# A graph layer's first product as seven block products, and norms applied one stage after their statistics

## The chip, the core and the metric

The kernel runs on one core of a Trainium2 chip. The metric is device time in microseconds for one launch; the table below has the runs. A core has TensorE (PE in the profile; its weight loads are PEld), VectorE (DVE), ScalarE (ACT), GpSimd (POOL) and SyncE (SP), each with an instruction queue of its own, and 16 DMA engines. All data is 32-bit float.

## The reference, cut to what matters

`x` is 128 graphs of 64 nodes with 256 features, `adj` their 64x64 weighted adjacency. Four layers follow each other, and each ends in `x = layernorm(x + layer(x, adj))`. Layer 0 takes five groups of the first 25 nodes (25, 9, 7, 6 and 6 nodes). For each group `g`:

```
def _graph_conv(x, adj, W, b):
    A = adj + eye
    norm_adj = dinv[:, :, None] * A * dinv[:, None, :]
    return relu(norm_adj @ (x @ W) + b)
...
h     = _graph_conv(x_g, adj_g, W1[g], b1[g])      # 256 -> 512
out_g = _graph_conv(h,   adj_g, W2[g], b2[g])      # 512 -> 256
fused[:, idx] += norm_w[g] * out_g
```

Nodes 25 to 63 belong to no group: in layer 0 they only get the layer norm. Layer 1 is one such convolution, layer 2 a polynomial in the adjacency, and layer 3 five rounds of messages and a GRU cell, which take most of the time.

## The kernel before, in words

**Units.** Layer 0 is cut into 16 units (`Unit`, L42; `UNITS`, L61), numbered from 0. A unit is up to four tiles of up to 126 rows of one group; a tile's rows are all nodes of the group in some graphs. The groups come in the order 1, 2, 3, 4, 0: units 0 to 2 are group 1 (504, 504 and 144 rows), 3 and 4 group 2 (448 each), 5 and 6 group 3 (504, 264), 7 and 8 group 4 (504, 264), 9 to 15 group 0 (500 each, the last 200). Units 6 and 8 have tiles of 126, 126 and 12 rows.

**Stages of a unit.** `load0` (L345) loads adjacency and features. `prep` (L367) forms the normalized adjacency of each tile on VectorE, with a power on GpSimd (`inv_sqrt`, L116), transposes it on TensorE (L399) and evicts it as `AT` (L403). `aggregate` (L406) multiplies features and adjacency (L413) and copies the result to `ag0`, which has 2 blocks of 128 features by the unit's rows as columns. `hidden` (L421) is the first product: `hg` has 4 blocks of 128 hidden features; each is the sum of two products of a 128x128 block of `W1` with a block of `ag0` (L428), 8 matmuls over all columns, then a relu with bias on ScalarE (L432). `support` (L436) is the second product, two tiles to a PSUM bank (L444), copied by ScalarE (L450). `add` (L457) multiplies by the adjacency again (L466) with a relu (L470) and adds into `F`. For group 0, `finish` (L491) transposes back, adds and norms, and stores to `xa` (L514).

**Order.** TensorE's order is the order of the code (`manual_schedule`, L332). The other engines' orders are set by a planner that works with priorities; `high_priority` raises them, and `issue_after(ins)` keeps instructions behind `ins` on that engine. `evictions[-1]` is the last L403 traced. The loop at L581 goes over stages `i`, each with `add(i-1)`, `aggregate(i+1)`, `support(i)`, `finish(i-1)`, `prep(i+2)`, `hidden(i+1)`. From stage 10 on, `early_stage` weaves the start of layers 1 and 2 for the first two chunks (`mid`, L220) in between; its L210 is the first to read `xt`.

**PSUM.** There are eight banks, five in the pool `pg` and three in `pt`; `psum0` (L181) takes five of eight in turn from `pg` and three from `pt`.

**Other nodes.** Groups of up to four nodes pass through `load_others` (two stages ahead), `others` (L522) and `store_others` (L527) to `xb` in DRAM. `norm_stats` (L128) takes statistics on VectorE and a power on GpSimd (L139), `norm_apply` (L146) subtracts and scales on VectorE (L154). `load_x` (L194) reads `xa` and `xb` back by SyncE (L199); it is first called at stage 10. The last two groups are normed in stage 9 and stored in stage 10.

**Weights.** `load_first` (L549) and `load_second` (L552) bring a group's `W1` and `W2`, 512 KB each, by one DMA on SyncE, into tiles that hold all five groups; all are loaded by stage 4.

**Layer 3** already forms a product of 2x2 blocks by seven block products: `sums` (L714) on GpSimd, `factors` (L681) on VectorE, and `Gates` (L722), whose `product(i)` multiplies (L737), copies partial sums out of PSUM on ScalarE (L754), and adds on VectorE (L756, L760, L766).

Of the kernel before, what the change touches and what calls it, by code (L numbers as in the profile page):

```python
# [68 lines left out]
def gnn_stack(  # L69
# [117 lines left out]


    def load_adj(c):
        a64 = keep.tile([128, NP, N], F32, name="a64", bufs=2)  # L190
        nc.sync.dma_start(a64, av[c])
        adjs[c] = a64
# [142 lines left out]
    with ExitStack() as c0:  # L335
        w0 = c0.enter_context(tc.tile_pool(name="w0", bufs=1))
        work = c0.enter_context(tc.tile_pool(name="work0", bufs=1))
        W1 = w0.tile([128, NG, 2, HID], F32, name="W1")
        W2 = w0.tile([128, NG, 4, D], F32, name="W2")

        F = w0.tile([128, 2, B, NE], F32, name="F")

        loads, A, AG, HG, S2, Z, XO = {}, {}, {}, {}, {}, {}, {}

# [75 lines left out]

        def hidden(i):  # L421
            u = UNITS[i]
            ag0 = AG.pop(i)
            hg = keep.tile([128, 4, 512], F32, tag="NI", name="hg", bufs=2)
            for e in range(4):
                p = psum0("ph")[:, : u.cols]
                for k in range(2):
                    nc.tensor.matmul(  # L428
                        p, W1[:, u.g, k, e * 128 : (e + 1) * 128], ag0[:, k, : u.cols], start=k == 0, stop=k == 1
                    )  # L430
                relus.append(
                    nc.scalar.activation(hg[:, e, : u.cols], p, AF.Relu, bias=b1[:, u.g * 4 + e : u.g * 4 + e + 1])  # L432
                )
            HG[i] = hg

        def support(i):  # L436
            u = UNITS[i]
            hg, s2 = HG.pop(i), []
            for v in range(0, len(u.tiles), 2):
                p = psum0("ps").rearrange("p (t d) -> p t d", t=2)  # L440
                ts = range(v, min(v + 2, len(u.tiles)))
                for t in ts:
                    for e in range(4):
                        nc.tensor.matmul(  # L444
                            p[: u.rows[t], t - v, :], hg[:, e, u.off[t] : u.off[t] + u.rows[t]], W2[:, u.g, e, :],
                            start=e == 0, stop=e == 3,
                        )
                sv = work.tile([TR, 2, D], F32, name="s2", bufs=4)
                if u.rows[ts[0]] == u.rows[ts[-1]]:
                    nc.scalar.copy(sv[: u.rows[v], : len(ts), :], p[: u.rows[v], : len(ts), :])  # L450
                else:
                    for t in ts:
                        nc.scalar.copy(sv[: u.rows[t], t - v, :], p[: u.rows[t], t - v, :])
                s2 += [sv[:, t - v, :] for t in ts]
            S2[i] = s2
# [66 lines left out]
        def others(i):  # L522

            with tc.issue_after(evictions[-1].ins):
                layernorm(XO[i], n=XO[i].shape[1])

        def store_others(i):  # L527
            t = XO.pop(i)
            nc.sync.dma_start(xb[:, NP * i : NP * i + t.shape[1], :], t)

# [18 lines left out]
        def load_first(g):  # L549
            nc.sync.dma_start(W1[:, g], w1[g].rearrange("(k p) e -> p k e", p=128))  # L550

        def load_second(g):  # L552
            nc.sync.dma_start(W2[:, g], w2[g].rearrange("(k p) e -> p k e", p=128))

# [21 lines left out]
        def stage(f, i, first=0):  # L576
            if first <= i < NU:
                f(i)

        g0 = next(i for i, u in enumerate(UNITS) if u.g == 0)  # L580
        for i in range(-2, NU + 1):  # L581
            if i >= 0:
                stage(load0, i + 3)
            stage(add, i - 1)
            if i:
                stage(aggregate, i + 1)
            early_stage(i, 0)
            stage(support, i)
            if not i:
                aggregate(1)  # L590
            if i == NU:
                folds = [products(0, q) for q in range(3)]
            stage(finish, i - 1, g0)
            early_stage(i, 1)
            if i == -1:

                hidden(0)
                with tc.issue_after(evictions[0].ins):
                    prep(1)
            else:  # L600
                stage(prep, i + 2)
                stage(hidden, i + 1)
            if i == -2:
                load0(1, powers[0])
                load_second(1)
                load0(2, powers[0])
                load_first(2)
            elif i == -1:
                load_second(2)
                load_first(3)  # L610
            elif i == 0:
                load_second(3)
            elif i < 5:
                (load_first, load_second)[(i - 1) % 2]((4, 0)[(i - 1) // 2])
            early_stage(i, 2)
# [56 lines left out]


    WHH = work.tile([128, 3, 7, 128], F32, name="WHH")
    V = [work.tile([128, 3, 7, 128], F32, name=f"V{l}") for l in range(L)]

    raw21 = []

    raw21 = []

    def factors(w):  # L681

        nc.vector.tensor_sub(w[:, :, 5, :], w[:, :, 4, :], w[:, :, 0, :])
        nc.vector.tensor_sub(w[:, :, 2, :], w[:, :, 1, :], w[:, :, 5, :])

    def fold():
# [7 lines left out]
        for l in range(L):  # L694
            for q in range(3):
# [12 lines left out]
                if q == 2 and l == 0:  # L708
                    nc.vector.tensor_add(WHH[:, :, 4, :], w21, WHH[:, :, 3, :])
                    nc.vector.tensor_sub(WHH[:, :, 6, :], WHH[:, :, 0, :], w21)  # L710
                    factors(WHH)
                yield

    def sums(a, name):  # L714

        t = work.tile([128, 4, H], F32, tag="T" + name, name="T" + name, bufs=2)
        nc.gpsimd.tensor_sub(t[:, 0:2, :], a[:, :, H:], a[:, 0, :].rearrange("p (s n) -> p s n", s=2))  # L717
        nc.gpsimd.tensor_sub(t[:, 2, :], a[:, 1, H:], t[:, 0, :])
        nc.gpsimd.tensor_sub(t[:, 3, :], a[:, 1, :H], t[:, 2, :])
        return t  # L720

    class Gates:  # L722

        def __init__(self, C, sides, name):
            self.C, self.sides, self.name = C, sides, name
            self.copies = {}

        def multiply(self, bank, i):  # L730
            for g, side in enumerate(self.sides):
                for m, (w, q, a, t) in enumerate(side):
                    rhs = {
                        1: a[:, 0, :H], 2: a[:, 1, :H], 3: a[:, 1, H:], 4: t[:, 3, :], 5: t[:, 0, :], 6: t[:, 2, :],
                        7: t[:, 1, :],
                    }[i]
                    nc.tensor.matmul(  # L737
                        bank[:, g, :], w[:, q, i - 1, :], rhs, start=i in (1, 2, 5) and g == 0 and m == 0,
                        stop=m == len(side) - 1, skip_group_check=True,
                    )  # L740

        def bank(self, s):
            return pg.tile([128, 2, H], F32, tag="pg", name=f"p{s}{self.name}")

        def product(self, i):
            C = self.C
            if i == 1:
                self.a = self.bank("a")
            if i in (1, 6, 7, 4):
                self.multiply(self.a, i)  # L750
                if i != 4:
                    c = self.copies[i] = work.tile([128, 2, H], F32, tag="copy", name=f"c{i}", bufs=4)
                    with tc.high_priority():
                        nc.scalar.copy(c, self.a)  # L754
                if i == 7:
                    nc.vector.tensor_add(C[:, :, 1, H:], self.d, self.copies.pop(7))  # L756
            elif i == 2:
                b = self.bank("b")
                self.multiply(b, i)
                nc.vector.tensor_add(C[:, :, 0, :H], b, self.copies.pop(1))  # L760
            else:
                if i == 5:
                    self.d = self.bank("d")
                self.multiply(self.d, i)
                if i == 3:
                    nc.vector.tensor_add(C[:, :, 0, H:], self.d, self.copies.pop(6))  # L766

    class Chunk:
# [12 lines left out]
        def state_of_layer2(self, k):  # L781
# [4 lines left out]
            if not k:  # L786
                self.th = sums(self.hT, "h")

        def messages(self, h=None):
            self.agg = gather(self.xt if h is None else h, self.A01, "agg", work, "agg", 2)  # L790
            self.ta = sums(self.agg, "a")

        def rz(self, i):
            if i == 1:
                self.RZ = keep.tile([128, 2, 2, NP * 128], F32, tag="RZ", name="RZ", bufs=2)
                self.g = Gates(
                    self.RZ, [[(WHH, q, self.hT, self.th), (V[self.l], q, self.agg, self.ta)] for q in (0, 1)], "rz"
                )
# [11 lines left out]
        def n(self, i):  # L810
            if i == 1:
                self.NI = keep.tile([128, 2, 2, NP * 128], F32, tag="NI", name="NI", bufs=2)
                self.gn = Gates(
                    self.NI, [[(V[self.l], 2, self.agg, self.ta)], [(WHH, 2, self.hT, self.th)]], "n"
                )
# [61 lines left out]
        def turn(self, k):  # L877
# [9 lines left out]
            if not last:  # L887
                with tc.high_priority():
                    nc.scalar.copy(self.h[:, :, f], pv)
                if not k:  # L890
                    self.th = sums(self.hT, "h")
            else:
# [159 lines left out]
```

## Time and profile before

| what | value |
|---|---|
| three runs | 2195.18, 2197.6, 2195.16 us (median 2195.18) |
| profiled run, its span | 2195.32 us, 2193.5 us |
| layer 0 | about the first 300 us of the span |
| TensorE, share of busy time, 0 to 100 us and 100 to 200 us | 97%, 100% |
| VectorE, 100 to 200 us | 48% |
| ScalarE, 100 to 200 us | 37% |
| GpSimd, 100 to 200 us | 16% |
| DMA, mean share of 16 engines, 0 to 20 us and 160 to 180 us | 0.87, 0.15 |

A row of the view of groups has line, engine, operation, output and input tiles, shape and count, then busy time and the mean of one in ns, then the idle time before it and what ended it. A row of the timeline has the start, the time from the first start to the last end, and the count. `SPq` is SyncE's queue, in which DMAs are issued. A window's row has its bounds, its length, then busy time and count of PE, PEld, DVE, ACT and POOL, then TensorE's granted clock, the share of the DMA engines and GB/s.

### The profile page before, as it was taken

To read this page: it belongs to the slowest core of one execution; us is meant where nothing else is said; L and a number is where in the kernel's file an instruction comes from. 1 tells how busy PE (TensorE), PEld (TensorE's weight loads), DVE (VectorE), ACT (ScalarE), POOL (GpSimd) and SP (SyncE) were. 2 spreads that over 40 slices of the span, in tenths; PEclk is the share of its full clock that TensorE was granted. 3 is DMA by queue.
4 is the path that set the end of the run, shared out by engine and by line. 5 is a ranking of instruction groups with operands and counts; after the bars stand their busy time and mean duration, and the time that the engine had idled before them with its cause. 6 is when DMAs were issued, how large, how long until landed. Compare 5 with 4: busy or idle time off the path is not lost.

```text
span 2193.5 us, 30145 instructions
## 1 busy us (share of the span) xinstructions
PE 2177.2 (99%) x11542; PEld 1907.7 (87%) x11542; DVE 1362.9 (62%) x3060; ACT 1001.2 (46%) x1839; POOL 571.2 (26%) x621
## 2 busy tenths in 40 slices
PE   9999999999999999999999999999999999999997
PEld 6777888898988889888989888888898898888886
DVE  3445666566766576666666676657666666556546
ACT  3333334544544554444444454445444544455453
POOL 3211131222332222222322222222322222222221
PEclk9999999999999999999999999999999999999998
DMA  6532110000100010000000010001000000000000
GB/s 166 180 120 67 49 37 3 1 3 1 42 1 3 1 41 2 3 1 20 22 3 1 1 42 1 3 1 42 1 1 1 20 10 1 1 10 11 1 1 20
DMA packets 54172, 51.12 MB, mean 23 GB/s; under 512 B 20878, under 2 KB 49036, under 8 KB 54028
## 3 DMA queue, kind: packets, MB, share of 16 engines
q1 hardware_dynamic: 49664, 43.96, 6.5%
q0 software_dynamic: 1936, 4.83, 0.8%
q8 instruction: 91, 1.49, 0.3%
q10 hardware_dynamic: 2428, 0.41, 0.1%
q14 instruction: 53, 0.43, 0.1%
HBM read 32.40 MB, written 16.78 MB: 22 GB/s over the span
## 4 chain that ended last, share of the span: by engine, by line
PE 96%; DVE 1%; issue 1%; POOL 0%; ACT 0%; DMA 0%; SPq 0%; POOLq 0%; ACTq 0%; DVEq 0%
PE parz L737 25%; PE pdrz L737 12%; PE pan L737 12%; PE pa L210 9%; PE pbrz L737 6%; PE pdn L737 6%; PE ps L444 4%; PE ph L428 4%; PE pT L778 4%; PE pbn L737 3%; PE pd L288 3%; PE pd L309 2%; PE pa L413 1%; PE po L466 1%; PE pf L562 1%
## 5 line engine op out<-in xcount | busy, mean ns | idle before, releaser
L754 ACT COPY c<-parz 128x512 f32<-128x512 f32 x240 | 140.6, 586 | 323.3 <-PE parz L737 322.7
L737 PE MATMUL parz<-Th,WHH 128*128 128x256 f32 x960 | 285.9, 379 | 0.3 <-ACT c L754 0.3
L737 PE MATMUL parz<-Ta,V 128*128 128x256 f32 x960 | 285.6, 379 | 0.0
L717 POOL TENSOR_TENSOR Th<-hn 128x512 f32<-128x512 f32 x64 | 81.5, 1273 | 777.6 <-DVE hn L839 603.2
L836 ACT ACTIVATE NI<-NI,bih 128x512 f32<-128x512 f32 (+1 forms) x162 | 115.9, 715 | 203.8 <-DVE NI L831 203.7
L754 ACT COPY c<-pan 128x512 f32<-128x512 f32 x237 | 139.0, 586 | 149.7 <-PE pan L737 149.6
L737 PEld LDWEIGHTS parz<-Ta,V 128*128 128x128 f32 x960 | 182.4, 190 | 24.8
L737 PEld LDWEIGHTS parz<-Th,WHH 128*128 128x128 f32 x960 | 176.2, 190 | 21.4 <-ACT c L754 0.7
L808 ACT ACTIVATE RZ<-RZ,brz 128x512 f32<-128x512 f32 x160 | 116.0, 726 | 138.9 <-DVE RZ L766 138.9
L717 POOL TENSOR_TENSOR Ta<-agg 128x512 f32<-128x512 f32 x80 | 102.1, 1277 | 261.0 <-ACT agg L214 261.0
L766 DVE TENSOR_TENSOR RZ<-pdrz,c 128x512 f32<-128x512 f32 x80 | 55.0, 688 | 173.8 <-PE pdrz L737 173.8
L139 POOL TENSOR_TENSOR rs<-ve,mhalf 128x4 f32<-128x4 f32 (+3 forms) x67 | 68.4, 1021 | 304.3 <-DVE ve L137 243.9
L737 PE MATMUL pan<-Ta,V 128*128 128x256 f32 x474 | 141.2, 380 | 0.0
L737 PE MATMUL pan<-Th,WHH 128*128 128x256 f32 x474 | 141.0, 379 | 0.0
L760 DVE TENSOR_TENSOR NI<-pbn,c 128x512 f32<-128x512 f32 x79 | 54.6, 691 | 127.4 <-PE pbn L737 110.2
L210 PEld LDWEIGHTS pa<-A,h 128*128 128x128 f32 x1024 | 124.4, 192 | 3.3
L210 PE MATMUL pa<-A,h 128*128 128x128 f32 x1024 | 124.7, 275 | 0.0
L756 DVE TENSOR_TENSOR NI<-pdn,c 128x512 f32<-128x512 f32 x79 | 54.4, 689 | 112.8 <-ACT c L754 112.8
L837 DVE TENSOR_TENSOR RZ<-hn,NI 128x512 f32<-128x512 f32 (+1 forms) x129 | 87.7, 680 | 49.5 <-ACT NI L836 49.5
L839 DVE TENSOR_TENSOR hn<-RZ,NI 128x512 f32<-128x512 f32 (+1 forms) x161 | 109.6, 681 | 1.8
L838 DVE TENSOR_TENSOR RZ<-RZ 128x512 f32<-128x512 f32 (+1 forms) x161 | 109.4, 680 | 1.8
L444 PE MATMUL ps<-W,hg 128*125 128x256 f32 (+5 forms) x464 | 103.6, 380 | 0.3 <-ACT v L315 0.3
(217 smaller groups left out, 5051.9 us busy)
## 6 DMA issues: line engine op xcount, KB each, us to landing
out_dram<-xt SPq DMA_DIRECT2D x32, 256.0 KB
W<-in_w_dram SPq DMA_DIRECT2D x10, 512.0 KB
xt<-xb SPq DMA_DIRECT2D x32, 156.0 KB
xo<-in_x_dram SPq DMA_DIRECT2D x9, 512.0 KB
xb<-xo SPq DMA_DIRECT2D x9, 512.0 KB
xt<-xa SPq DMA_DIRECT2D x32, 100.0 KB
xg<-in_x_dram SPq DMA_DIRECT2D x25, 125.0 KB
xa<-xg SPq DMA_DIRECT2D x25, 125.0 KB
```

What stands on the lines that cost most here:

```text
L210: nc.tensor.matmul(p[:, q * 128 : (q + 1) * 128], src[:, q, k * 128 : (k + 1) * 128], m[:, q, :], start=True, stop=True)
L428: nc.tensor.matmul(p, W1[:, u.g, k, e * 128 : (e + 1) * 128], ag0[:, k, : u.cols], start=k == 0, stop=k == 1)
L444: nc.tensor.matmul(p[: u.rows[t], t - v, :], hg[:, e, u.off[t] : u.off[t] + u.rows[t]], W2[:, u.g, e, :], start=e == 0, stop=e == 3,)
L717: nc.gpsimd.tensor_sub(t[:, 0:2, :], a[:, :, H:], a[:, 0, :].rearrange("p (s n) -> p s n", s=2))
L737: nc.tensor.matmul(bank[:, g, :], w[:, q, i - 1, :], rhs, start=i in (1, 2, 5) and g == 0 and m == 0, stop=m == len(side) - 1, skip_group_ ...
L754: nc.scalar.copy(c, self.a)
L778: nc.tensor.transpose(p[:, q * 128 : (q + 1) * 128], src(q, k), ident)
L808: nc.scalar.activation(RZ[:, q, 0, :], RZ[:, q, 0, :], AF.Sigmoid, bias=b[0])
L836: nc.scalar.activation(n, n, AF.Tanh, bias=bih[:, 4 + j : 5 + j])
L837: e.tensor_sub(d, self.hT[:, j, f], n)
L838: e.tensor_mul(d, d, z)
L839: e.tensor_add(self.hn[:, j, f], d, n)
```

## The change

**First product.** `hidden` becomes a generator. For units with `2 < i < g0 + 2` (`g0` = 9, `hidden` gets unit `i+1`), and at least 256 columns, it forms the 4x2 blocks of weights as two 2x2 products side by side, each by seven block products over half of the columns: `sums` makes four combinations of `ag0`'s quarters on GpSimd, `factors` three combinations of weight blocks on VectorE, and `Gates` (moved to the head of the kernel, with the bank and the pool passed in) runs the products in the order 1, 6, 2, 5, 7, 4, 3. Products 1, 6, 7 and 4 add up in one PSUM bank, 5 and 3 in a second, 2 has a third. After 1, 6 and 7 ScalarE copies the bank; after 2, 7 and 3 VectorE adds a copy and a bank into `hg`, and relus of half the columns follow in place; after 4 they read the bank. The first product runs before the last pair of tiles of the stage's `support`, 6, 2, 5 and 7 after `prep`, 4 between `add` and `aggregate` of the next stage, 3 after that `aggregate`. Other units keep 8 products at the old place.

**Weights.** `W1` of a group has room for seven blocks per half of its outputs, two groups at a time, with one block apart (`W21`); four DMAs with 512-byte runs bring it. `W2` has three buffers. Groups 3, 4 and 0 load `W1` in stages 2, 4 and 6, and `W2` of groups 4 and 0 in stages 3 and 5; `factors` runs in stages 2, 3, 5 and 7.

**Other nodes.** `others` keeps the statistics, and `store_others`, one stage later, applies them ahead of the store, behind the last eviction.

```diff
-            for e in range(4):
-                p = psum0("ph")[:, : u.cols]
-                for k in range(2):
-                    nc.tensor.matmul(
-                        p, W1[:, u.g, k, e * 128 : (e + 1) * 128], ag0[:, k, : u.cols], start=k == 0, stop=k == 1
-                    )
...
+            if not seven or u.cols < H:
+                for _ in range(5):
+                    yield
+                for e in range(4):
...
+                return
+            h = u.cols // 2
+            with tc.high_priority():
+                t = sums(ag0, work, "0", 1)
+            C = hg.rearrange("p (g j) n -> p g j n", g=2)[:, :, :, : u.cols]
+            taken[0] += 1
+            g7 = Gates(C, [[(w, g, ag0, t)] for g in range(2)], work, lambda s: psum0("ph" + s))
+            for m in (1, 6, 2, 5, 7, 4, 3):
+                yield
+                with tc.high_priority():
+                    g7.product(m)
+                for g in range(2):
...
+                    if m in (2, 7, 3, 4):
+                        nc.scalar.activation(C[:, g, j, f], C[:, g, j, f] if m != 4 else g7.a[:, g, :], AF.Relu, bias=b(2 * g + j))
...
         def others(i):
 
             with tc.issue_after(evictions[-1].ins):
-                layernorm(XO[i], n=XO[i].shape[1])
+                NO[i] = norm_stats(XO[i], n=XO[i].shape[1])
 
         def store_others(i):
             t = XO.pop(i)
+            with tc.issue_after(evictions[-1].ins):
+                norm_apply(t, *NO.pop(i), n=t.shape[1])
             nc.sync.dma_start(xb[:, NP * i : NP * i + t.shape[1], :], t)
...
         def load_first(g):
-            nc.sync.dma_start(W1[:, g], w1[g].rearrange("(k p) e -> p k e", p=128))
+            W1[g] = w0.tile([128, 2, 7, 128], F32, tag="W1", name=f"W1{g}", bufs=2)
+            W21[g] = w0.tile([128, 2, 128], F32, tag="W21", name=f"W21{g}", bufs=2)
+            v = w1[g].rearrange("(k p) (q e) -> p k q e", p=128, q=2)
+            for k in range(2):
+                nc.sync.dma_start(W1[g][:, :, k, :], v[:, k, :, :128])
+            nc.sync.dma_start(W21[g], v[:, 0, :, 128:])
+            nc.sync.dma_start(W1[g][:, :, 3, :], v[:, 1, :, 128:])
...
             stage(add, i - 1)
+            next(cur, None)
             if i:
                 stage(aggregate, i + 1)
+            for _ in cur:
+                pass
             early_stage(i, 0)
-            stage(support, i)
+
+            nxt = hidden(i + 1, 2 < i < g0 + 2) if 0 <= i + 1 < NU else iter(())
+            if 0 <= i < NU:
+                for last in support(i):
+                    if last and i:
+                        next(nxt, None)
+                        next(nxt, None)
...
             else:
                 stage(prep, i + 2)
-                stage(hidden, i + 1)
+                for _ in range(3):
+                    next(nxt, None)
+            next(nxt, None)
+            cur = nxt
```

## The prediction

> **What bounds the kernel now.** I read the engines' busy time first, then the chain that ended last.
>
> ```profile
> span 2193.5 us, 30145 instructions
> PE 2177.2 (99%) x11542; PEld 1907.7 (87%) x11542; DVE 1362.9 (62%) x3060; ACT 1001.2 (46%) x1839; POOL 571.2 (26%) x621
> ...
> PE 96%; DVE 1%; issue 1%; POOL 0%; ACT 0%; DMA 0%; SPq 0%; POOLq 0%; ACTq 0%; DVEq 0%
> ```
>
> TensorE is busy for 99% of the span and is 96% of the chain. The view of waits for TensorE between 19 and 300 us, which holds nearly the whole of layer 0, has a single entry of 0.3 us. So inside layer 0 matmul time is the time: what is taken from it comes off the end, unless a new wait takes its place. Next the order of TensorE's work for two units:
>
> ```profile
> 150.71 0.70 PE L399 MATMUL pT<-ident,A 125*125 125x125 f32 x4
> 151.25 6.88 PE L428 MATMUL ph<-ag,W 128*128 128x500 f32 x16
> 157.96 1.88 PE L466 MATMUL po<-AT,s 126*128 126x126 f32 x12
> 159.77 2.05 PE L413 MATMUL pa<-AT,xg 125*128 125x125 f32 x16
> 161.66 7.07 PE L444 MATMUL ps<-W,hg 128*125 128x256 f32 x32
> ```
>
> One stage is prep (L399), the first product of the next unit (L428), add (L466), aggregate (L413), support (L444). Starts matter, not durations, which overlap: L428 owns 151.25 to 157.96. Each f32 matmul has two records, so 8 products are 16 records. Last, the windows of the eight stretches of L428 that the change touches:
>
> ```profile
> 72.37:78.39 6.02, 6.02 (x19) 3.05 (x18) 4.50 (x23) 2.31 (x4) 1.56 (x2) 1.00 0.33 110
> 89.28:96.14 6.86, 6.86 (x17) 3.15 (x17) 4.62 (x23) 2.46 (x4) 2.03 (x2) 1.00 0.48 159
> 107.18:110.75 3.57, 3.57 (x19) 3.05 (x17) 2.85 (x16) 1.85 (x4) 0.73 (x1) 1.00 0.33 116
> 151.25:157.96 6.71, 6.71 (x18) 3.04 (x17) 5.39 (x21) 2.03 (x3) 2.14 (x2) 1.00 0.05 8
> ...
> sum 47.00, PE 47.00 PEld 24.52 DVE 37.21 ACT 17.05 POOL 12.44; mean PE 5.88 PEld 3.07 DVE 4.65 ACT 2.13 POOL 1.56
> ```
>
> The first number after each window is its length, then TensorE's busy time: full in each. The clock, third from the end, is 1.00 throughout. The sum of the eight is 47.00 us.
>
> [...] 500 columns take 6.71/16 = 419 ns a record, 264 columns 3.57/16 = 223 ns; the slope is 0.83 ns a column and 2.9 ns are left. [...] L413's 125-column records stand 112 ns apart though each has a weight load of 192 ns beside it. [...] a subtraction of 128x384 took 0.87 us at 313.31, beside GpSimd's sums, and 0.54 us at 315.11.
>
> **The change, part by part.**
>
> Fewer products. The condition "2 < i < g0 + 2" with g0 = 9 makes units 4 to 11, counted from 0, eight units in all (the short description names five to eleven). Each has 14 matmuls of half the columns for 8 of all: 7/8 of the columns. Gain 47.00/8 = 5.88 us. The cost is 28 records for 16, 12 more in each of 8 units at 2.9 ns = 0.28 us. **Net −5.60 us.** Bounds: records of 504 columns stand 429 ns apart, 6 ns above the line through 500 and 264; if half-length ones lose that too, two units give 0.1 us each more (−5.9). If the 132-column records of units 6 and 8 meet a floor (125 columns already take 112 ns, 5 ns over the line), 2 x 28 x 5 ns = 0.3 us goes (−5.3). L444's 256-column records, 6.91/32 = 216 ns, speak for the line.
>
> Work added beside TensorE, in each such unit: three ScalarE copies of a bank (586 ns each by L754's 512 columns), eight relus of half length for four (677 ns at 500 columns and 480 at 264 give 0.47 us at 250, so 3.7 us for 2.7): +2.8 us. VectorE: three additions at 0.69 us (L760) = 2.1 us. GpSimd: sums of 1.27 + 0.73 + 0.73 us (the rows of L717 to L719) = 2.7 us. A stage is some 18 us long. In it VectorE has 10 to 12 us, ScalarE 7 to 8, GpSimd 2 to 5; all fit. Four groups get weight sums, four VectorE operations of 256 elements a partition, 0.4 us each by L391's 417 ns at 252 columns: 1.7 us a group, off the path, ready a stage ahead. I book nothing for throughput.
>
> Waits. Three places have a product close to its reader. (a) The seventh product (3) ends just before support. Its addition (0.1 to 0.2 us to start, 0.69) and first relu (0.47) take 1.5 us; it fills the second half of the columns, which the second pair of tiles reads, 6.91/2 = 3.45 us later. Cover 1.9 us. In units 6 and 8 the half, 132 columns, ends inside tile 1, which is reached after 8 records = 1.7 us; the chain is 0.2 + 0.42 + 0.1 + 0.37 = 1.1 us; cover 0.6 us. (b) Product 7 overwrites the bank that the copy of 6 reads: two products, 1.7 us, or 0.9 in units 6 and 8, over about 0.8 us. (c) Three banks are held longer than four were. The number taken in a stage stays at four with the one skipped; walked through in the code's order with the spacings above, the bank that is taken again soonest was last written 1.3 us before (the second bank of aggregate for unit 8, after add for unit 6), and its eviction (L470) takes 0.57 us at 264 columns. Lower bound nothing, upper bound half a microsecond in each unit = 4 us. **Taken: +0.4 us**, mainly units 6 and 8, where VectorE must take the addition at once.
>
> Weights. Group 1 comes by four DMAs of 512 B runs for one of 2 KB runs. SyncE's issue was 0.58 us; three more push the queue behind it (adjacency of unit 1, second weights, unit 2, x loads) by 1.7 us. VectorE received unit 1's adjacency at 13.77 and had its blocks ready at 16.87; their transposes are due at 19.25, so there are 2.4 us of cover. The first product waited at 12.39 not for weights but for ScalarE, which stood until 10.46 on a DMA of the biases; that can come earlier or later when the weights' packets change. [...] Against that, group 3's 512 KB leave the start. Bounds −0.5 (the 0.48 us wait) to +1.5; **taken +0.1**. Later groups' loads wait for a buffer of a group two earlier, behind which SyncE has loads due a stage or more later; first use is at least a stage off: nothing.
>
> Norms of the other nodes. The same VectorE operations, a stage later. What goes is VectorE's wait in the queue for GpSimd's power, 7.9 us before L154 in layer 0; VectorE isn't the bound, so no gain. But the last two groups' norms (7 operations, 2.5 us by the spacing of 0.34 us) now come after the eviction of unit 12:
>
> ```profile
> 177.54 0.32 SPq L529 DMA_DIRECT2D xb<-xo  x1
> 181.28 0.77 SPq L199 DMA_DIRECT2D xt<-xb  x2
> 196.51 1.31 SPq L199 DMA_DIRECT2D xt<-xa  x3
> 206.90 1.95 PE L210 MATMUL pa<-AT,xt 128*128 128x128 f32 x16
> ```
>
> The last store now went out at 177.54; the loads that read it were back in time for L210 at 206.90. The eviction (L403) was at 188.04. With the norm of unit 9 beside it, the stores leave between 192 and 196, the loads about 200 to 202 [...], and land about 204, at most 2 to 3 us later. Due, less the product saved, at 206.1. Behind the stores on SyncE wait exactly these loads. Bounds 0 to +2.5; **taken +0.2**.
>
> Sum: −5.60 + 0.4 + 0.1 + 0.2 = −4.9 us, a span of 2188.6. Runs take 1.8 us more than the profiled span (2195.32 for 2193.5), and the median is 2195.18: **2190.3 us**.
>
> **The rivals.** *Part of it is given back* (waits (a) to (c) at 0.2 to 0.4 us a unit, or a start or a first gather at its upper bound): 1.5 to 3 us more, 2191.8 to 2193.3. For it: several covers under 1 us. Against: layer 3 runs this same scheme with 0.3 us of such waits.
>
> *VectorE's queue stands before product 3.* Statistics and norm of other nodes, 1.9 + 1.4 us at 89.80 to 94.20, follow the eviction; if they, held up by additions that wait for TensorE, stand ahead of product 3's addition with a delay d, six units lose d − 1.9 and two lose d − 0.6. It costs what is gained (5.6) at d of about 2.3 us, and at 3.3 it is 6 x 1.4 + 2 x 2.7 = 13.8 us: **2203.4, slower**. For it: [...] in units with weight sums 8 to 9 us of VectorE work between eviction and product 3, some 8.7 us of TensorE work apart. Against: the additions are issued at high priority, and VectorE idles for 7.5 us before L403 now.
>
> *Shorter matmuls don't take less* (a floor at 250 columns, or the branch not taken): 2195. L444 speaks against it.
>
> **How the numbers follow.** Forecast 0.58 (2188.6 to 2191.0), part given back 0.25, queue 0.13, no saving 0.04. A measurement tells about 0.2%, 4.4 us, from no change: faster means under 2190.8. Of the forecast's 0.58 I count 0.55 there; the rest of it, the part given back and no saving make 0.32; the queue 0.13. The range begins at 2188.5 (the bound of −5.9 with no new waits and the start's gain of 0.5 would be 2188.8, and I allow 0.3 under it) and goes to 2195.2, which leaves out the queue alone and about 0.05 around the ends.
>
> **What would show it.** L428's windows for units 4 to 11 should add up to 41.4 us instead of 47.0; TensorE's waits between 19 and 300 us should stay under 1 us. Waits of L444 for ScalarE's relus would be (a) or the queue, of the new products for a copy (b), of L210 for xt the norms. A first product later than 12.4 us would be the weights.

## The result, and the profile after

| kernel | median of runs, us | lowest to highest | runs | profiled span, us |
|---|---|---|---|---|
| before | 2195.35 | 2195.16 to 2197.6 | 6 | 2193.5 |
| changed | 2203.64 | 2201.8 to 2207.12 | 6 | 2202.8 |

The changed kernel takes 1.0038 of the time before, 95% interval 1.0025 to 1.0051: about 8 us slower, where 4.9 us faster was forecast. The profiled execution of the changed kernel is 0.95 us above its median, so the two profiles are 9.3 us apart, and the account below is of these 9.3. Lines of the changed kernel have moved: L224 is the matmul of a block product (L737 before), L242 its copy, L193 to L196 the weight sums, L202 to L204 the sums on GpSimd, L278 the gather (L210), L338 the product ahead of it (L270), L346 the one behind (L278), L467 and L471 transposes and eviction (L399, L403), L481 aggregate, L504 the first product by eight, L532 support, L554 add, L619 the store of other nodes, L267 the loads that read it, L659 the products for layer 3's weights (L562), L807 to L811 loads of these weights.

The head of the page and its chain:

```profile
span 2202.8 us, 30490 instructions
PE 2178.1 (99%) x11638; PEld 1926.5 (87%) x11638; DVE 1389.7 (63%) x3100; ACT 1016.1 (46%) x1895; POOL 590.7 (27%) x645
...
PE 95%; DVE 2%; issue 1%; DMA 1%; POOL 0%; ACT 0%; SPq 0%; POOLq 0%; DVEq 0%; ACTq 0%
```

TensorE looks as full as before, with 2178.1 us busy for 2177.2, although it has an eighth less to do in eight products. DMA and VectorE have a larger share of the chain. The waits of TensorE in the first 320 us say where (a row: who waits for whom, us in total, times, longest):

```profile
PE pha L224 <- ACT c L242: 2.5, 1, 2.5
PE pa L278 <- DMA xt<-xb: 2.3, 1, 2.3
```

and from 300 us to the end:

```profile
PE pf L659 <- DVE V L823: 3.8, 1, 3.8
```

Three waits make 8.6 us. The timeline of TensorE at these places shows why that isn't all; the bracket at the end of a row is the idle time before it, and what ended it:

```profile
113.60 3.44 PE L481 MATMUL pa<-AT,xg 126*128 126x126 f32 x16
...
208.96 3.61 PE L278 MATMUL pa<-AT,xt 128*128 128x128 f32 x16 [2.34 <-DMA xt<-xb]
...
325.39 3.42 PE L659 MATMUL pf<-ih,wl 128*128 128x256 f32 x8 [3.82 <-DVE V L823]
```

The gather's 16 records (L278) take 3.61 us; the page before had 1.95 us for them. Windows over the three places, for TensorE alone, with the granted clock third from the end:

```profile
113.31:116.73 3.42, 3.42 (x18) 0.50 0.64 188
116.73:118.00 1.27, 1.27 (x11) 1.00 0.89 327
...
208.89:212.30 3.41, 3.34 (x16) 0.50 0.27 75
324.94:328.35 3.41, 2.96 (x7) 0.50 0.00 0
```

At each of the three places the granted clock was 0.50 ("half clock" below) for 3.4 us; in the third this began 0.45 us before the wait ended. By an estimate from these windows, half of the 2.96 to 3.42 us in which TensorE worked at it is lost, so each wait costs 1.5 to 1.7 us more than it lasts. The rows agree: 16 records of L481 take 3.44 us there and 1.95 at 79.27, L278's 3.61 for the 1.95 before, and 8 of L659 3.42 us there and 1.89 at 329.09. The profile counts work at half clock as busy (3.42 of 3.42 us in the first window): that is why the busy time hides it.

**The account.** I compare starts of the same rows in both profiles. Before the change:

```profile
55.75 6.19 PE L428 MATMUL ph<-ag,W 128*128 128x448 f32 x16
...
206.00 1.06 PE L270 MATMUL pp<-poly,An 128*128 128x128 f32 x8
...
208.68 1.06 PE L278 MATMUL pp<-poly,An 128*128 128x128 f32 x8
```

and after it:

```profile
56.32 6.19 PE L504 MATMUL ph<-ag,W 128*128 128x448 f32 x16
...
205.56 1.06 PE L338 MATMUL pp<-poly,An 128*128 128x128 f32 x8
...
212.41 1.06 PE L346 MATMUL pp<-poly,An 128*128 128x128 f32 x8
```

What the products save on their own is read from the last experiment, which has no wait in the second stretch: 5.53 us.

| stretch | before | changed | difference |
|---|---|---|---|
| start to unit 3's first product, still by eight | 55.75 | 56.32 | +0.57 |
| from there to the product ahead of the gather (L270, L338) | 150.25 | 149.24 | −1.01, which is −5.53 + 4.52 |
| from there to the one behind the gather (L278, L346) | 2.68 | 6.85 | +4.17 |
| from there to the end | 1984.82 | 1990.39 | +5.57 |
| span | 2193.5 | 2202.8 | +9.3 |

So the saving was had, and three late arrivals cost 4.5, 4.2 and 5.6 us. The 4.5 is a remainder; read directly, unit 6's rows from add (108.49) to product 3 (116.88) take 8.39 us, and 4.02 in the last experiment, which is 4.4 us of it. Each late arrival has a chain that can be read.

**Unit 6: weights.** SyncE's queue and then VectorE's and ScalarE's, in timelines:

```profile
105.11 1.58 SPq L644 DMA_DIRECT2D W<-in_w_dram  x2
106.74 0.94 SPq L646 DMA_DIRECT2D W<-in_w_dram  x1
```

```profile
111.03 0.42 DVE L193 TENSOR_TENSOR W<-W,W 128x256 f32<-128x256 f32 x1 [3.46 <-DMA W<-in_w_dram]
111.37 0.42 DVE L248 TENSOR_TENSOR hg<-phb,c 128x264 f32<-128x264 f32 x1
```

```profile
111.83 0.70 ACT L520 ACTIVATE hg<-hg,b 128x132 f32<-128x132 f32 x2 [4.06 <-DVE hg L248]
112.44 0.35 ACT L242 COPY c<-pha 128x264 f32<-128x264 f32 x1
```

The sums of group 4's weights (L193) stood at the head of VectorE's queue from 107.57 to 111.03, waiting for weights that SyncE issued only from 105.11 on. Behind them stood product 2's addition (L248), behind that on ScalarE the relu, and behind the relu the copy of product 7 (L242), for whose bank TensorE's product 4 waited until 112.94. The wait names ScalarE, which was only the last link of a chain from SyncE by the DMA and VectorE.

**The gather: norms.** Timelines of SyncE's queue in the changed kernel:

```profile
199.10 0.82 SPq L619 DMA_DIRECT2D xb<-xo  x2
199.97 2.20 SPq L267 DMA_DIRECT2D xt<-xa  x2
205.07 1.18 SPq L267 DMA_DIRECT2D xt<-xb  x3
```

The last two groups' norms ran on VectorE at 192.07 to 198.18, spread between statistics, finish's norm and product additions. Their stores left at 199.10, the loads that read them at 205.07, and TensorE began at 208.96.

**Layer 3's weights: a place in SBUF.** GpSimd's waits between 300 and 320 us:

```profile
POOL wh L807 <- DMA xa<-xg: 4.6, 1, 4.6
```

The load of a weight block of layer 3 waited for a store of layer 0's output. The text of neither was changed. But the two can have a place in SBUF in common. By the tile sizes in the two kernels the group-wise weight tiles take 28672 B a partition instead of 40960; the new tiles `T0` and `copy` take the 12288 B that this frees but come after `xg`, so `xg` lies 12288 B lower. Then another of its six buffers, read by a later store, can lie where layer 3's `wh21` is put. No view shows addresses, so this is an inference, which the third experiment tests. The load went out at 313.32 (before at 305.04), the sums on VectorE waited 6.0 us for it (3.2 before), and the products' additions stood behind them.

### The profile page after: what moved, and what is told of

Its sections match the earlier page's. It is cut to its first block, busy times and chain, and to the rows that moved or that the text cites. A ratio compares the mean times of both kernels' runs of the same rounds, so it can differ in the third digit from the quotient of the medians.

```text
span 2202.8 us, 30490 instructions
## 1 busy us (share of the span) xinstructions
PE 2178.1 (99%) x11638; PEld 1926.5 (87%) x11638; DVE 1389.7 (63%) x3100; ACT 1016.1 (46%) x1895; POOL 590.7 (27%) x645
## 3 DMA queue, kind: packets, MB, share of 16 engines
q8 instruction: 92, 1.51, 0.3%
## 4 chain that ended last, share of the span: by engine, by line
PE 95%; DVE 2%; issue 1%; DMA 1%; POOL 0%; ACT 0%; SPq 0%; POOLq 0%; DVEq 0%; ACTq 0%
PE parz L224 25%; PE pdrz L224 12%; PE pan L224 12%; PE pa L278 9%; PE pbrz L224 6%; PE pdn L224 6%; PE ps L532 4%; PE pT L843 4%; PE pbn L224 3%; PE pd L377 3%; PE pd L356 3%; PE ph L504 2%; PE pa L481 1%; PE po L554 1%; PE pha L224 1%
## 5 line engine op out<-in xcount | busy, mean ns | idle before, releaser
L202 POOL TENSOR_TENSOR Th<-hn 128x512 f32<-128x512 f32 x64 | 81.4, 1272 | 778.1 <-DVE hn L906 603.1
L242 ACT COPY c<-parz 128x512 f32<-128x512 f32 x240 | 140.6, 586 | 323.2 <-PE parz L224 322.6
L224 PE MATMUL parz<-Th,WHH 128*128 128x256 f32 x960 | 285.9, 379 | 0.3 <-ACT c L242 0.3
L224 PE MATMUL parz<-Ta,V 128*128 128x256 f32 x960 | 285.5, 379 | 0.0
L242 ACT COPY c<-pan 128x512 f32<-128x512 f32 x237 | 138.9, 586 | 149.6 <-PE pan L224 149.6
L224 PEld LDWEIGHTS parz<-Ta,V 128*128 128x128 f32 x960 | 182.4, 190 | 24.8
L224 PEld LDWEIGHTS parz<-Th,WHH 128*128 128x128 f32 x960 | 176.2, 190 | 21.4 <-ACT c L242 0.7
L202 POOL TENSOR_TENSOR Ta<-agg 128x512 f32<-128x512 f32 x80 | 102.2, 1278 | 260.1 <-ACT agg L282 260.1
L224 PE MATMUL pan<-Ta,V 128*128 128x256 f32 x474 | 141.2, 380 | 0.0
L224 PE MATMUL pan<-Th,WHH 128*128 128x256 f32 x474 | 141.0, 379 | 0.0
L248 DVE TENSOR_TENSOR NI<-pbn,c 128x512 f32<-128x512 f32 x79 | 54.6, 692 | 127.8 <-PE pbn L224 110.2
L278 PEld LDWEIGHTS pa<-A,h 128*128 128x128 f32 x1024 | 124.4, 192 | 3.3
L278 PE MATMUL pa<-A,h 128*128 128x128 f32 x1024 | 124.6, 275 | 0.0
L532 PE MATMUL ps<-W,hg 128*125 128x256 f32 (+5 forms) x464 | 104.5, 380 | 0.3 <-ACT v L383 0.3
```

The source lines that it names most:

```text
L202: nc.gpsimd.tensor_sub(t[:, 0:2, :], a[:, :, h:], a[:, 0, :].rearrange("p (s n) -> p s n", s=2))
L224: nc.tensor.matmul(bank[:, g, :], w[:, q, i - 1, :], rhs, start=i in (1, 2, 5) and g == 0 and m == 0, stop=m == len(side) - 1, skip_group_ ...
L278: nc.tensor.matmul(p[:, q * 128 : (q + 1) * 128], src[:, q, k * 128 : (k + 1) * 128], m[:, q, :], start=True, stop=True)
L532: nc.tensor.matmul(p[: u.rows[t], t - v, :], hg[:, e, u.off[t] : u.off[t] + u.rows[t]], W2[u.g][:, e, :], start=e == 0, stop=e == 3,)
```

## The experiments

Each run has the kernel before beside it on the same chip; its medians were 2195.5 to 2195.7 us. All differences from it are under 1%, so the intervals are what tells them from noise. Theory: three late arrivals, each of which can be taken away alone.

### Unit 6's sums later

```diff
+            with tc.issue_after(thirds[-1].ins) if i == 6 else nullcontext(): i == 6 and factors(W1[4], W21[4])
...
-                    factors(W1[g], W21[g])
+                    i == 5 or factors(W1[g], W21[g])
```

`thirds[-1]` is the addition of product 3, after which nothing of the unit waits for VectorE.

> The weight sums of group 4 are queued behind the last addition of unit 6's first product, a stage later than in the changed kernel, and are otherwise the same. Theory A (three separate waits, each with about 3.4 us at half clock behind it): VectorE no longer stands 3.5 us on the load of W1 for group 4, TensorE's 2.5 us wait of product 4 of unit 6 for ScalarE's copy goes, and so does the half clock after it: 4.2 us less than the changed kernel's 2203.6, about 2199.4; the waits for xt and for V stay at about 2.3 and 3.8 us. Rival B (VectorE's queue is too full for the added work as a whole, with the other nodes' norms ahead of the additions): the wait of product 4 of unit 6 only shrinks or moves to another product, and the time stays within 1 us of 2203.6.

Measured: 2204.18 us (2203.44 to 2205.63), 1.0039 of before, interval 1.0027 to 1.0052. The expected gain failed. Unit 6's wait was gone, but the same chain stood one group later, in unit 8 with group 0's weights. VectorE's timeline:

```profile
138.78 0.42 DVE L193 TENSOR_TENSOR W<-W,W 128x256 f32<-128x256 f32 x1 [2.38 <-DMA W<-in_w_dram]
```

It kept TensorE for 1.4 us. The wait for `xt` grew to 3.0 us, and the half clock beside it lasted 6.8 us instead of 3.4. Removing one wait had only let the next be seen.

### Norms with their statistics again

```diff
-                NO[i] = norm_stats(XO[i], n=XO[i].shape[1])
+                layernorm(XO[i], n=XO[i].shape[1])
...
-            with tc.issue_after(evictions[-1].ins):
-                norm_apply(t, *NO.pop(i), n=t.shape[1])
```

> The other nodes' norms are applied in the stage of their statistics, as before; all else is as in the changed kernel. Theory A: only the wait of L278 for xt goes, 2.3 us and some 1.7 us of half clock behind it: about 2199.6, with the waits for unit 6's copy and for V unchanged. Rival B: with the norms out of the way the waits inside the first product go too, and the time falls by 7 us or more. Rival C (the added store order alone matters, not the norms): no change, 2203.6.

Measured: 2207.04 us (2205.57 to 2208.98), 1.0051, interval 1.0037 to 1.0064: by its median slower than the whole change (the two intervals overlap), where 2199.6 was expected. The wait for `xt` went, but units 6 and 8 got new ones, in support behind product 3's relu:

```profile
PE ps L532 <- ACT hg L520: 5.4, 2, 3.2
```

VectorE's timeline in unit 6 has the norm ahead of product 3's addition:

```profile
115.46 3.24 DVE L154 TENSOR_SCALAR xo<-xo,mv,rs 128x256 f32<-128x256 f32 x4 [0.90 <-POOL rs L139]
118.62 0.42 DVE L254 TENSOR_TENSOR hg<-phd,c 128x264 f32<-128x264 f32 x1
```

The norm waits 0.90 us for GpSimd's power, and its four operations take 3.24 us, while GpSimd's sums run from 115.39 to 118.23; in the kernel before, four took 1.38 us at 92.90, with GpSimd idle from 92.86 to 94.50. That the sums make the norms longer isn't shown by this alone: no run here takes the sums away to test it. Either way they stand ahead of product 3's addition, so delaying the norms is what keeps VectorE's queue clear for product 3; only for the last two groups it is wrong.

### Only the places in SBUF

```diff
         work = c0.enter_context(tc.tile_pool(name="work0", bufs=1))
...
+        work.tile([128, 4, H], F32, tag="T0", name="T0", bufs=1), work.tile([128, 2, H], F32, tag="copy", name="c0", bufs=4)
```

The two new tags get their places first, and by the sizes `xg` is back where it was; no instruction changes.

> The scratch tiles of the new first product (four sums and four copies, 12 KB a partition) are placed ahead of the x tiles in the pool, so that these come to lie at the addresses that they had in the kernel before; nothing else is changed. Theory A: the load of layer 3's weights (wh21) then overlaps x tiles whose last store is done earlier, GpSimd no longer waits 4.6 us for a store to xa, and TensorE's wait of 3.8 us for V goes with its half clock: 5.4 us less, about 2198.2. Rival D (the late weights come from the shift of the schedule, not from addresses): the wait for V stays and the time is within 1 us of 2203.6.

Measured: 2199.17 us (2196.28 to 2201.11), 1.0015, interval 1.0007 to 1.0023, some 4.5 us less than the changed kernel, where 5.4 was expected. As the theory had it, GpSimd's load has no wait and TensorE's wait for `V` at L659 is gone. Two waits of over 1 us are left between 19 and 320 us, and unit 6's has grown by 1.1 us, which is about what the gain falls short by:

```profile
PE pha L224 <- ACT c L242: 3.6, 1, 3.6
PE pa L278 <- DMA xt<-xb: 2.5, 1, 2.5
```

### The kernel before with late norms alone

The hunks of `others` and `store_others` were put into the kernel before.

> The kernel before with one part of the change alone: the other nodes' norms are applied one stage after their statistics. Theory A: the last two stores to xb leave after about 192 us for 177 and the first gather of xt at 207 us waits, though VectorE has less else to do here than in the changed kernel: 0 to 4 us more than before, about 2197 to 2199. Rival E (the late store matters only with the new additions on VectorE): 2195.3, no wait for xt.

Measured: 2195.58 us (2195.26 to 2195.8), 1.000, interval 0.9992 to 1.0008. Theory A failed and rival E was right: there is no wait for `xt`, as the stores left at 194.44 and the loads at 201.54, in time for 207.05. In the changed kernel VectorE was busy for 6.00 of the 6 us from 192 to 198, here for 4.41, and the stores were 4.7 us later. The delay of the norms did harm only with the fuller VectorE of the changed kernel.

### Both groups' sums later, with the places mended

```diff
+            with tc.issue_after(thirds[-1].ins) if i in (6, 8) else nullcontext(): i in (6, 8) and factors(W1[{6: 4, 8: 0}[i]], W21[{6: 4, 8: 0}[i]])
...
-                    factors(W1[g], W21[g])
+                    i > 3 or factors(W1[g], W21[g])
```

> The layout edit (T0 and the copies allocated first), and beside it the weight sums of both group 4 and group 0 issued after the third addition of units 6 and 8, a stage later than the change has them. Theory (three separate late arrivals, each worth its wait of 2.3 to 3.8 us and about 1.6 us of half clock after it): neither unit 6 nor unit 8 has a wait of TensorE for ScalarE's copy, the gather's wait of some 2.5 us for xt stays, and the time falls by about 4 us from the layout edit's 2199.2, to 2195.2. Rival (VectorE's queue is simply full: a wait moves from unit to unit wherever the sums go, as it did from unit 6 to unit 8 when group 4's alone were moved): a wait of over 1 us appears in another unit of layer 0 and the time stays at 2198 to 2199.5.

Measured: 2194.41 us (2192.28 to 2195.56), 0.9991, interval 0.9983 to 1.0000. As the theory had it: no wait in units 6 and 8, and 4.8 us less than with the places alone. The gather's wait remained, and its timeline was a surprise:

```profile
203.12 2.02 PE L278 MATMUL pa<-AT,xt 128*128 128x128 f32 x16 [2.17 <-DMA xt<-xb]
```

After 2.17 us the clock stayed at 1.00 and the 16 records took 2.02 us; in the changed kernel they took 3.61 after 2.34. The profile doesn't stand for all runs of this kernel: its 13 runs have spans of 2190.2 to 2190.8 us (six, the profiled one among them) or of 2192.3 to 2193.5 (seven). Half clock after the same wait in the seven would fit the gap of some 2 us, by the 1.66 us that it cost the gather in the changed kernel, but none of them was profiled.

### The weights by another queue

```diff
-                nc.sync.dma_start(W1[g][:, :, k, :], v[:, k, :, :128])
+            e = nc.gpsimd if g in (4, 0) else nc.sync
+            for k in range(2): e.dma_start(W1[g][:, :, k, :], v[:, k, :, :128])
```

and so for the other two loads; places in SBUF mended, sums where the change has them.

> The layout edit, and the four loads of the first weights of groups 4 and 0 issued on GpSimd's queue instead of SyncE's; the weight sums stand where the change has them, in the same order on VectorE. Theory (VectorE waited for weights whose issue stood in SyncE's queue behind loads of adjacency and x): the weights are issued some 20 us earlier, right after the product that frees their buffer; VectorE's first weight sum waits under 0.5 us for its DMA, TensorE's wait for ScalarE's copy in unit 6 is under 0.5 us, and the time is about 2195.2, as with late sums. Rival (the four sums themselves, some 1.7 us of VectorE ahead of the additions, delay the copy): the DMA is early and the wait in unit 6 stays over 1 us, time 2198 to 2199.

Measured: 2196.05 us (2194.46 to 2199.86), 1.0004, interval 0.9995 to 1.0012. Three of group 4's four loads went out at 83.44 to 87.09 instead of 105.11 to 107.68, VectorE's sums waited for nothing (L193 at 106.57 follows the eviction at 105.97 directly), and unit 6's wait was gone: SyncE's queue was the cause, not the sums as such. The time missed the expected 2195.2 by 0.9 us: part of the gain went into a new wait of 2.3 us, for which GpSimd's timeline gives the reason:

```profile
115.69 0.75 POOL L644 DMA_DIRECT2D W<-in_w_dram  x1
116.47 0.73 POOL L203 TENSOR_TENSOR T<-ag,T 128x252 f32<-128x252 f32 x1
117.13 0.73 POOL L646 DMA_DIRECT2D W<-in_w_dram  x1
117.88 0.73 POOL L204 TENSOR_TENSOR T<-ag,T 128x252 f32<-128x252 f32 x1
118.55 1.24 POOL L123 TENSOR_TENSOR d0r<-d0s,mhalf 126x2 f32<-126x2 f32 x2
```

Issuing group 0's loads takes 0.73 to 0.75 us each on GpSimd, ahead of the power (L123) that unit 8's adjacency needs; VectorE's blocks came late, TensorE's transposes waited for them until 120.63 (2.29 us), and half clock followed, with 0.50 in the windows from 122.63 to 124.63.

### The last norms at once

```diff
-                NO[i] = norm_stats(XO[i], n=XO[i].shape[1])
+                NO[i] = norm_stats(XO[i], n=XO[i].shape[1]); i > 7 and norm_apply(XO[i], *NO[i], n=XO[i].shape[1])
```

This once with the places alone, and once with both groups' late sums besides.

> The layout edit, and only the last two groups of other nodes normed in the stage of their statistics. Theory: their stores leave SyncE some 15 us earlier, the loads that read them are back before the first gather, TensorE's wait for xt (2.3 us and half clock after it) is gone, that in unit 6 stays; about 2195.2. Rival (late stores aren't the cause, since the kernel before with late norms alone had no such wait: SyncE's queue or shared bandwidth holds the loads): the wait stays above 1 us and the time at 2198 to 2199.5.

> The previous kernel, and the last two groups of other nodes normed in the stage of their statistics (unit 10's stage; the earlier groups stay a stage behind), so that their stores leave SyncE before unit 12's eviction. Theory: with all three late arrivals gone TensorE's waits between 19 and 300 us add to under 1 us, and the gain of the products, some 4.9 us less what the start loses, is left: 2191 (2190 to 2192), under the kernel before by 0.2%. Rival (half clock and queues hit something else once these are gone, the saving can't be had): 2194 to 2196, with a new wait over 1 us to be named.

Measured: 2198.63 us (2197.47 to 2199.57), 1.0012, interval 1.0006 to 1.0019, and 2193.41 us (2192.5 to 2195.42), 0.9990, interval 0.9984 to 0.9997. Both missed, by 3.4 and 2.4 us; the first lies in its rival's range, though the wait that the rival kept is gone. The wait for `xt` went in both: late stores were its cause. But both have a wait of 2.25 us for unit 12's adjacency blocks instead. In the second kernel:

```profile
PE pT L467 <- DVE A L459: 2.3, 1, 2.3
```

and VectorE's timeline, where the norms now stand ahead of these blocks:

```profile
177.45 1.83 DVE L154 TENSOR_SCALAR xo<-xo,mv,rs 128x256 f32<-128x256 f32 x3
...
184.66 0.68 DVE L459 TENSOR_TENSOR A<-ae,block 125x500 f32<-125x500 f32 x1
```

In the kernel with both groups' late sums and late norms, the same L459 began at 180.86. The norms are wrong in either place, for two different readers.

### The last norms between the two readers

```diff
-            with tc.issue_after(evictions[-1].ins):
+            with tc.issue_after((blocks if i > 7 else evictions)[-1].ins), tc.high_priority() if i > 7 else nullcontext():
                 norm_apply(t, *NO.pop(i), n=t.shape[1])
```

`blocks[-1]` is the last L459. Places mended, both groups' sums late.

> The kernel with the late sums of both groups and the layout edit, and the last two groups of other nodes normed right after unit 12's adjacency blocks (VectorE's product that makes A) instead of after its eviction a product later, as the change has it, or in the stage of their statistics, where they stood before those blocks and kept TensorE's transposes waiting for 2.3 us. Theory (each wait is a matter of what stands ahead of what in VectorE's queue; with the norms behind the blocks and ahead of finish both readers are served): neither the gather's wait for xt nor the transposes' wait for the blocks; TensorE's waits between 19 and 300 us under 0.5 us; the saving of the products, 4.9 us, less some tenths at the start, is left: 2191.0 (2190.4 to 2191.8), span 2188.5 to 2189.5. Rival (VectorE is full in the stages of units 11 and 12, so the 2.5 us of norms show wherever they stand): a wait of about 2 us before finish or before the aggregate of unit 12, and 2193 to 2194.5.

Measured: **2190.31 us** (2189.49 to 2190.84), 0.9975 of before, interval 0.9964 to 0.9985. It is 5.3 us faster than the kernel before and some 13 us faster than the changed one, and slightly under what was expected: the median by 0.1 us, the span by 0.9. The page's head, and all waits of TensorE in the first 320 us:

```profile
span 2187.6 us, 30498 instructions
```

```profile
PE pw L626 <- DVE zero L623: 1.5, 1, 1.5
PE pT L843 <- DVE V L823: 0.9, 1, 0.9
PE pa L481 <- DVE AT L471: 0.8, 1, 0.8
PE ps L532 <- ACT v L383: 0.3, 1, 0.3
```

These four were there before the change. VectorE's timeline shows the seven norms in one piece behind the blocks, and SyncE's the stores and loads:

```profile
181.13 0.68 DVE L459 TENSOR_TENSOR A<-ae,block 125x500 f32<-125x500 f32 x1
181.72 2.35 DVE L154 TENSOR_SCALAR xo<-xo,mv,rs 128x256 f32<-128x256 f32 x7
183.99 1.28 DVE L594 TENSOR_TENSOR xg<-pse,xg 125x512 f32<-125x512 f32 x2
```

```profile
183.78 0.80 SPq L619 DMA_DIRECT2D xb<-xo  x2
187.47 0.76 SPq L267 DMA_DIRECT2D xt<-xb  x2
```

The stores leave 15.3 us earlier than in the changed kernel. The rows that bound the second stretch of the account are these:

```profile
55.50 6.19 PE L504 MATMUL ph<-ag,W 128*128 128x448 f32 x16
...
200.22 1.06 PE L338 MATMUL pp<-poly,An 128*128 128x128 f32 x8
```

Between unit 3's first product and the product ahead of the gather lie 144.72 us, where it was 150.25 before: 5.53 us less, with no wait in between. That is the saving that the account above uses.

## Why the prediction was wrong

The time was 2203.64 us; 2190.3 was predicted, with 2195.2 as the upper end. Point by point:

- **Fewer products, −5.60 us.** Right: 5.53 us in the kernel without waits. The rows at 250 columns stand 210 to 213 ns apart there, those at 132 columns 113 ns, as the straight line had it; no floor down to 132 columns. The bound of −5.9 was a slip: two units at 0.1 us each make −5.8. The sign named for it, L428's windows, was a worse measure: in the same kernel the stretches of L224 add to 42.1 us instead of the 41.4 named, and the other rows of the account's second stretch are 0.7 us shorter in sum, which makes up for it.
- **Throughput of the other engines, nothing.** Right for the average, and not the question.
- **Waits (a) to (c), +0.4 us.** Too much: all three kernels with late sums and mended places show none of them in layer 0. The sign of (b), a wait for a copy, did appear, but the copy was the end of another chain.
- **Weights, +0.1 us, later groups nothing.** This is the first step that failed: "behind which SyncE has loads due a stage or more later; first use is at least a stage off: nothing", and the sums "off the path, ready a stage ahead". Group 4's weights stood in SyncE's queue behind loads of later stages until 105.11, though unit 4 had done with their buffer before 82; on GpSimd's queue they went at 83.44. And first use isn't the product but the sum, which stands in VectorE's queue ahead of additions that TensorE waits for. What was booked at nothing cost 4.5 us in unit 6. Of the start, booked at +0.1, the profile has +0.57 in the changed kernel and −0.25 in the last one; the named sign, a first product after 12.4 us, came (12.97) without any wait for weights. The start goes with the warm-up on zeros at the head of the kernel, whose matmuls stand 0.85 us apart at first and 0.43 later: the change of pace came at about 4.4 us before and 7.5 in the changed kernel, and the warm-up took 6.82 and 8.38 us.
- **Norms, +0.2 us, at most +2.5.** The second step: the mechanism was right, its size wrong. Stores were to leave at 192 to 196 and the loads to land at about 204, by an estimate. With late norms alone they left at 194.44; in the changed kernel at 199.10, where VectorE was busy without a break from 192 to 198, and TensorE began at 208.96. The wait was 2.34 us, near the upper bound, and the half clock that went with it made it 4.2.
- **What had no step at all.** Tiles that got smaller moved another tile's place, and a load three layers later waited for a store that read it: 5.6 us. And no price was put on the clock after a wait: by the estimate above, half clock makes 1.5 to 1.7 us of each of the three.
- **The rivals.** "VectorE's queue stands before product 3" gave 2203.4, and the time is near, but by chance: in the changed kernel it was product 2's addition in one unit, behind a DMA, and over half of the loss lies outside layer 0's products. With the norms back in their old place its mechanism did decide units 6 and 8. The argument against it, that additions are issued at high priority, failed: in unit 6 the addition L248, at high priority, stood behind L193 and started at 111.37, after L193's wait of 3.46 us for its DMA.

The forecast of 2190.3 us is the time of the last experiment's kernel, in which the added work makes nothing wait. That the two agree to 0.01 us is luck: that kernel gains 5.3 us on the kernel before beside it (2195.62), and 4.9 was forecast from 2195.18. The arithmetic of the matmuls was right; that nothing would wait was wrong three times.

## What to carry to other kernels

For each instruction that a change puts into an engine's queue, ask what it can itself wait for, a DMA's place in its own queue included, and who stands behind it; "off the path" is true only of work that can't block a queue (here sums that waited 3.46 us for a DMA held an addition behind them). After a change of tile sizes, compare the tiles' places and look for waits in parts that weren't touched, since a reused place can be a dependency that no line of code shows (here, as inferred and then tested, 5.6 us). When a wait is taken away and the time doesn't fall, look for the next one of the same kind before giving up the theory: here only the kernel with all three gone, and none new, showed the whole gain.

## What the runs showed of the hardware

A short wait of TensorE cost more than its length in some of these profiles and not in others. Between 19 and 335 us, the eleven waits of 2.29 to 3.9 us and one of 2.21 us (unit 8 with all norms at once) had a granted clock of 0.50 in their last part or after them. Those of 1.4, 1.51, 2.03 and 2.17 us had 1.00 throughout, and so had two of 2.25 us (unit 12's transposes), though they were longer than the one of 2.21. So the length alone doesn't say it.

The half clock lasted 3.4 us in the changed kernel, in each of its three places (from 113.31, 208.89 and 324.94 us on). Three slow stretches in other profiles (unit 6 with norms at once, unit 6 with the last norms at once, the gather with group 4's sums late) lasted 6.8 us, here the last of them:

```profile
205.74:212.56 6.82, 5.87 (x27) 0.50 0.38 103
```

What decides whether the clock falls, and for how long, isn't shown. For a wait of about 2.2 us both were seen, so one profile of a kernel with such a wait need not show its usual time: that of the kernel with late sums and mended places, whose gather waited 2.17 us at a clock of 1.00, has a span of 2190.3 us, and seven of this kernel's 13 runs had 2192.3 to 2193.5.
